# A four-layer convolution kernel: the statistics pass of the quantised convolution reordered by hand, and layer 0's output maximum taken image by image

## The chip, the core and the metric

The kernel runs on one core of one Trainium2 chip. The metric is the device time of one execution in microseconds (us), from the first to the last instruction. A second figure used below is the granted TensorE clock, as a share of full speed, which the profile lists.

The core has five instruction streams. PE (TensorE) multiplies matrices into the accumulator memory PSUM, which has eight banks of 128 x 512 fp32. DVE (VectorE) and ACT (ScalarE) work elementwise. POOL (GpSimd) does cross-partition maxima and memsets here. SP (SyncE) only issues DMA transfers, which 16 DMA engines carry out between HBM and the on-chip memory SBUF. Each stream is executed in its own order and waits on semaphores for the others.

## What is computed

The input x has shape (4, 16, 512, 512): four images of 16 channels. Four layers follow one another.

```python
# layer 0: depthwise 3x3 convolution, windowed attention (8 x 8 windows, 2 heads), MLP, residuals
x = layer0(x)
# layer 1: 8-bit fake quantisation of input and weights, 3x3 convolution, batch norm, clip
step = max(abs(x)) / 127                      # over the whole tensor
xq = clip(round(x / step), -127, 127) * step
y = conv3x3(xq, wq)
mean, var = y.mean(axis=(0, 2, 3)), y.var(axis=(0, 2, 3))
x = clip(y * inv + (beta - mean * inv), 0, 6)  # inv = gamma / sqrt(var + eps)
# layer 2: x + conv3x3(relu(conv3x3(x)))
# layer 3: x + mlp(conv3x3(x)), hidden width 128
```

Layer 1 has two dependences on the whole tensor. The quantisation step needs the largest magnitude of layer 0's output, and the batch norm needs the mean and variance of the convolution's output. So the input of layer 1 is read twice: once for the statistics, once for the result.

## The kernel before

**Layer 0** is `window_attention` (L138). It makes 64 steps. Each step handles a column band 64 wide of all four images; two steps (an even and an odd n) share one input tile and one output tile `xo` of [128, 4 images, 8 rows, 128 columns]. The order of PE, DVE, ACT and SP is written out by hand (`tc.manual_schedule`, L451): what stands first in the program runs first on its engine. Within a step come eight blocks of scores, exponentials and weighted sums (L482 to L498), the projection (L500), and then the MLP of 16 pieces (L510 to L517), between which the depthwise convolution of step n + 2 is spread. `output` (L425) adds the MLP's result to the residual and writes one image's part of `xo` (L430). Its fourth call for a step is made only in the next step, behind that step's first transposes and scores (L477). After both halves, `store` (L435) takes the maximum of |xo| over the whole tile into one column of `peak` with one VectorE reduction (L437), and issues 32 DMAs into the HBM tensor `x1` (L444), eight per image. At the end, a bound on the scores is reduced to a flag (L526 to L537) that SyncE loads (L538); a fallback, `attention_block`, runs only if the flag is zero.

**The statistics pass** is `quant_conv` (L857). Its own order is left to the scheduler. It first quantises the weights: a load of 98 KB (L880), a maximum over the partitions on GpSimd (L872), a step and its reciprocal, and the rounding by adding and subtracting 12582912 (L883, L884). The same function `step_of` turns `peak` into the input's step. Then it walks over 65 tiles `lx` of [128, 4, 512] fp32 (1 MB each; row pairs of the four images, from four strips that lie 128 rows apart). For each tile, `load` (L898) issues four DMAs of 256 KB (L964), scales in place on VectorE (L901), and rounds to bf16 on ScalarE (L902) into one of three ring tiles `lq`. There are three buffers for `lx`. For each of 64 output tiles, 96 small matmuls (L980, four by four at a time on 32 x 32 blocks) convolve two neighbouring ring tiles into four PSUM banks, and four `bn_stats` (L913) read one bank each:

```python
load(0)
for mm in range(M):
    load(mm + 1)
    p = [ps.tile([P, W], F32, tag="p", name=f"lp{mm}_{b}") for b in range(B)]
    for turn in _turns():
        _conv_turn(nc, p, cq, (ring[mm % 3], ring[(mm + 1) % 3]), *turn)
    for b in range(B):
        nc.vector.bn_stats(stats[:, mm * B + b, :], p[b])
```

After the loop the 256 partial statistics are aggregated (L929), summed over the strips with two matmuls (L918), and turned into a `scale` and a `shift` (L947) by a chain of small instructions.

**The tail** is `conv_tail` (L988), again in an order written by hand (L1164, which comes behind the first definitions). It reads `x1` again, quantises tile by tile (`scaled` L1042 on VectorE, `rounded` L1045 on ScalarE, one row of four at a time), and carries the layers 1, 2 and 3 as a pipeline over tiles: `done0` (L1050) applies `scale` and `shift` to the layer 1 convolution and makes z. Two load buffers (tag "x") and two output buffers (tag "o") are in use, each 1 MB, besides rings of padded tiles for the layers' intermediates. It starts with the tiles -2 and -1, which lie partly outside the image, and 0 (L1176).

Of the kernel before, what the change touches and what calls it, by code (L numbers as in the profile page):

```python
# [24 lines left out]
P = 128  # L25
# [75 lines left out]
@with_exitstack  # L101
def conv_chain(ctx: ExitStack, tc: tile.TileContext, x, mats, vecs, cqs, cws, hots, out):
    nc = tc.nc
    const = ctx.enter_context(tc.tile_pool(name="const", bufs=1))
    dram = ctx.enter_context(tc.tile_pool(name="dram", bufs=1, space=DRAM))


    x1 = dram.tile([B, (S + 1) * 2 * M, C, W], F32, name="x1")
    zero = const.tile([C, W], F32, name="zero")
    nc.vector.memset(zero, 0.0)  # L110
    for b in range(B):
        nc.sync.dma_start(x1[b, 0], zero)
        nc.sync.dma_start(x1[b, H + 1], zero)

    mat = const.tile([P, N_MAT], F32, name="mat")
    vec = const.tile([P, N_VEC], F32, name="vec")
    cw = const.tile([P, 3, 2, 3, 32], F32, name="cw")
    nc.sync.dma_start(mat, mats)
    nc.sync.dma_start(vec, vecs)
    nc.scalar.dma_start(cw, cws)  # L120

    def m(name):
        return mat[:, MAT_AT[name]]

    def v(name):
        return vec[:, VEC_AT[name]]

    peak = const.tile([P, HR // WS], F32, name="peak")

    safe = window_attention(tc, x, x1, hots, m, v, peak)  # L130
    with tc.If(safe == 0):
        attention_block(tc, x, x1, m, v, peak)
    quant = quant_conv(tc, x1, const, cqs, m, v, peak)
    conv_tail(tc, x1, out, cw, quant, m, v)


@with_exitstack
def window_attention(ctx: ExitStack, tc, x, x1, hots, m, v, peak):  # L138
# [286 lines left out]
    def output(y, xo, hids, u, half):  # L425
        b = bank(7)
        for vv, hd in hids:
            nc.tensor.matmul(b[quad(vv)], m("fc2"), hd, start=True, stop=True)  # L428
        at = BW * half
        nc.vector.tensor_tensor(  # L430
            xo[:, u, :, at : at + BW].rearrange("p a (j x) -> p a j x", x=WS),
            by_window(b), by_window(y[:, u]), ALU.add,
        )

    def store(xo, k):  # L435
        i, cb = divmod(k, NQ)
        nc.vector.tensor_reduce(  # L437
            peak[:, k : k + 1], xo, AX.XYZ, ALU.max, apply_absolute_value=True
        )
        for u in range(U):  # L440
            for vv in range(V):
                for w in range(2):
                    r = SR * (2 * vv + w) + WS * i
                    nc.sync.dma_start(  # L444
                        x1[u, r + 1 : r + 1 + WS, :, XW * cb : XW * cb + XW].rearrange(
                            "a c x -> c a x"
                        ),
                        xo[32 * vv + C * w : 32 * vv + C * w + C, u],
                    )
# [20 lines left out]
    for n in range(STEPS + 1):  # L470
# [4 lines left out]
        if last:  # L475

            output(*last)  # L477
            if n % 2 == 0:
                store(xo, n // 2 - 1)
# [30 lines left out]
        for i in range(13 * 4):  # L510
            q, rest = divmod(i - 4, 3)
            if i >= 4 and rest == 0 and q < 16:
                hids.append(hidden(y, q, n))
                if q in (5, 9):
                    output(y, xo, hids[q - 5 : q - 1], q // 4 - 1, n % 2)
# [5 lines left out]
        output(y, xo, hids[8:12], 2, n % 2)  # L521
        last = (y, xo, hids[12:], U - 1, n % 2)
# [333 lines left out]
@with_exitstack  # L856
def quant_conv(ctx: ExitStack, tc, x1, const, cqs, m, v, peak):  # L857

    nc = tc.nc
    one = ctx.enter_context(tc.tile_pool(name="l1c", bufs=1))
    rows = ctx.enter_context(tc.tile_pool(name="l1r", bufs=3))
    ps = ctx.enter_context(tc.tile_pool(name="l1p", bufs=8, space=PSUM))

    def step_of(columns, name):

        most = one.tile([P, 1], F32, name=f"most_{name}")
        nc.vector.tensor_reduce(most, columns, AX.X, ALU.max, apply_absolute_value=True)  # L870
        every = one.tile([P, 1], F32, name=f"every_{name}")
        nc.gpsimd.partition_all_reduce(every, most, P, bass_isa.ReduceOp.max)  # L872
        step = one.tile([P, 1], F32, name=f"step_{name}")
        nc.vector.tensor_scalar(step, every, 1.0 / QP, None, ALU.mult)
        inv = const.tile([P, 1], F32, name=f"inv_{name}")
        nc.vector.reciprocal(inv, step)
        return step, inv

    wf = one.tile([P, 6 * 32], F32, name="wf")
    nc.scalar.dma_start(wf, cqs)  # L880
    sw, iw = step_of(wf, "w")
    cq = const.tile([P, 2, 3, 32], BF16, name="cq")
    nc.vector.tensor_scalar(wf, wf, iw, ROUND, ALU.mult, ALU.add)  # L883
    nc.vector.tensor_scalar(  # L884
        cq.rearrange("p s d o -> p (s d o)"), wf, ROUND, None, ALU.subtract
    )
    unround = const.tile([P, 1], F32, name="unround")
    nc.vector.memset(unround, -ROUND)
    sx, ix = step_of(peak, "x")
    stats = one.tile([P, M * B, 6], F32, name="stats")  # L890

    ring = []
    for i in range(3):
        t = one.tile([P, S, WP], BF16, name=f"lq{i}")
        nc.gpsimd.memset(t[:, :, 0 : WP : WP - 1], 0.0)
        ring.append(t)

    def load(mm):  # L898
        t = rows.tile([P, S, W], F32, tag="x", name=f"lx{mm}")
        _load_pairs(nc, t, x1, mm)  # L900
        nc.vector.tensor_scalar(t, t, ix, ROUND, ALU.mult, ALU.add)  # L901
        nc.scalar.activation(  # L902
            ring[mm % 3][:, :, 1 : W + 1], t, AF.Identity, bias=unround
        )

    load(0)
    for mm in range(M):
        load(mm + 1)
        p = [ps.tile([P, W], F32, tag="p", name=f"lp{mm}_{b}") for b in range(B)]
        for turn in _turns():  # L910
            _conv_turn(nc, p, cq, (ring[mm % 3], ring[(mm + 1) % 3]), *turn)
        for b in range(B):
            nc.vector.bn_stats(stats[:, mm * B + b, :], p[b])  # L913


    def over_strips(col, name):
        p = ps.tile([P, W], F32, tag="p", name=f"pm_{name}")
        nc.tensor.matmul(p[:, 0:1], m("same"), col, start=True, stop=True)  # L918
        t = one.tile([P, 1], F32, name=f"os_{name}")
        nc.vector.tensor_scalar(t, p[:, 0:1], 1.0 / NS, None, ALU.mult)  # L920
        return t

    def mul(a, b, name):
        t = one.tile([P, 1], F32, name=f"mul_{name}")
        nc.vector.tensor_tensor(t, a, b, ALU.mult)
        return t

    own = one.tile([P, 2], F32, name="own")
    nc.vector.bn_aggr(own, stats.rearrange("p r s -> p (r s)"))  # L929
    mean = over_strips(own[:, 0:1], "mean")  # L930
    off = one.tile([P, 1], F32, name="off")
    nc.vector.tensor_tensor(off, own[:, 0:1], mean, ALU.subtract)
    spread = one.tile([P, 1], F32, name="spread")
    nc.vector.scalar_tensor_tensor(spread, off, off, own[:, 1:2], ALU.mult, ALU.add)
    var = over_strips(spread, "var")
    s = mul(sx, sw, "s")
    var = mul(mul(var, s, "v1"), s, "v2")
    nc.vector.tensor_scalar(var, var, BN_EPS, None, ALU.add)
    nc.scalar.activation(var, var, AF.Sqrt)
    inv = one.tile([P, 1], F32, name="inv")  # L940
    nc.vector.reciprocal(inv, var)
    inv = mul(inv, v("gamma"), "inv")
    scale = const.tile([P, 1], F32, name="scale")
    nc.vector.tensor_tensor(scale, inv, s, ALU.mult)
    shift = const.tile([P, 1], F32, name="shift")
    ms = mul(mean, scale, "ms")
    nc.vector.tensor_tensor(shift, v("beta"), ms, ALU.subtract)  # L947
    return ix, unround, cq, scale, shift
# [39 lines left out]
def conv_tail(ctx: ExitStack, tc, x1, out, cw, quant, m, v):  # L988
# [16 lines left out]
    ix, unround, cq, scale, shift = quant  # L1005
# [19 lines left out]
    nc.vector.tensor_scalar(edge_b1, v("edge"), v("l2_b1"), None, ALU.mult)  # L1025

# [9 lines left out]
    def load(mm):  # L1036
        loaded[mm] = ld.tile([P, S, W], F32, tag="x", name=f"tx{mm}")
        _load_pairs(nc, loaded[mm], x1, mm)

    def scaled(mm, s):  # L1040
        t = loaded[mm][:, s]
        nc.vector.tensor_scalar(t, t, ix, ROUND, ALU.mult, ALU.add)  # L1042

    def rounded(mm, s):
        nc.scalar.activation(  # L1045
            inner(qs(mm))[:, s], loaded[mm][:, s], AF.Identity, bias=unround
        )

# [92 lines left out]
    def group(conv, unit, between):  # L1141
# [18 lines left out]
        if unit:  # L1160
            waiting.append((*unit, hids))

    ctx.enter_context(
        tc.manual_schedule(  # L1164
            engines={
                mybir.EngineType.PE, mybir.EngineType.DVE, mybir.EngineType.Activation,
                mybir.EngineType.SP,
            }
        )
    )  # L1170

# [4 lines left out]
    for mm in (-2, -1, 0):  # L1176
        load(mm)
        if mm < 0:
            for s in range(S):
                scaled(mm, s)  # L1180
                rounded(mm, s)
    for t in range(-2, M + 7):
        if t + 3 <= M + 2:
            load(t + 3)
        new = [lambda s=s: scaled(t + 2, s) for s in range(S)]
        new += [lambda s=s: rounded(t + 2, s) for s in range(S)]
# [144 lines left out]
```

## Time and profile before

The times of three executions are 6926.55, 6930.18 and 6936.06 us; the median is 6930.18. The profiled execution has a span of 6931.8 us at a mean granted clock of 0.960. By stage:

| stretch (us) | stage | PE busy | DVE busy | ACT busy | clock | DMA share |
|---|---|---|---|---|---|---|
| 0 to 3628.5 | layer 0 | 3511.70 | 1599.29 | 2696.58 | 0.99 | 0.49 |
| 3628 to 4124 | statistics pass | 180.50 | 248.02 | 131.71 | 0.57 | 0.63 |
| 4124 to 6932 | tail | 2768.15 | 1330.46 | 1386.97 | 0.99 | 0.28 |

Some durations that matter, as the medians of their groups:

| instruction | count | one of it (ns) |
|---|---|---|
| scaling of a tile, DVE, L901 | 65 | 1268 |
| rounding of a tile, ACT, L902 | 65 | 2003 |
| bn_stats of a bank, DVE, L913 | 256 | 680 |
| aggregation, DVE, L929 | 1 | 7090 |
| maximum of xo, DVE, L437 | 32 | 4420 |

In the views of the trace, a row gives a start, a duration, the engine, the line in the kernel, what is written and read, and how many instructions were merged; square brackets give the idle time of the engine before it and the work whose end it waited for. Instructions of one group overlap by a little at their ends, so four bn_stats of 680 ns take less than four times that. In the waits, a row says who waited for whom, how long in total, how often, and the longest. In the stretches, the busy time of each engine is followed by the granted clock, the mean busy share of the DMA engines, and the rate in GB/s.

### The profile page before, as it was taken

How to read it: one execution, taken by the hardware profiler on the slowest of the kernel's cores; microseconds unless marked ns; L12 is line 12 of the kernel's file. 1: busy time of each engine (PE TensorE's matmuls, PEld its weight loads, DVE VectorE, ACT ScalarE, POOL GpSimd, SP SyncE). 2: the span in 40 equal slices, each digit the busy share in tenths (PEclk: the TensorE clock that was granted, in tenths of full speed). 3: DMA queues.
4: the chain of work that ended last, by engine and by line, in shares of the span. 5: the costliest groups of instructions: out<-in, count | busy, mean ns of one | idle time of the engine just before them, and what ended most of it. 6: DMA issues, size and time to landing. Idle time of an engine off the chain costs nothing. (4 is left out here: it accounts for less than half of the span.)

```text
span 6931.8 us, 317952 instructions
## 1 busy us (share of the span) xinstructions
PE 6460.4 (93%) x146976; PEld 3307.2 (48%) x146976; DVE 3177.8 (46%) x4550; ACT 4215.3 (61%) x5744; POOL 10.2 (0%) x51
## 2 busy tenths in 40 slices
PE   7999999999999999999983339999999999999999
PEld 4555555555555555555532224444444444444443
DVE  2444444444444444444434454444444444444444
ACT  4777777777777777777762234555555555555553
POOL 0000000000000000000000000000000000000000
PEclk9999999999999999999985559999999999999999
DMA  6455454545545454554327653222223222232221
GB/s 71 63 64 72 63 66 62 66 66 62 70 63 67 63 66 65 64 70 62 51 46 155 144 125 75 76 76 77 83 79 82 76 76 76 76 84 78 82 63 45
DMA packets 759438, 514.79 MB, mean 74 GB/s; under 512 B 354128, under 2 KB 648656, under 8 KB 749904
## 3 DMA queue, kind: packets, MB, share of 16 engines
q1 hardware_dynamic: 757808, 493.95, 40.2%
q8 instruction: 1154, 18.91, 1.3%
q14 instruction: 188, 1.54, 0.1%
q10 hardware_dynamic: 288, 0.39, 0.0%
HBM read 225.28 MB, written 134.48 MB: 52 GB/s over the span
## 5 line engine op out<-in xcount | busy, mean ns | idle before, releaser
L1115 PE MATMUL tb<-y,mat 32*32 32x512 f32 x16384 | 1685.8, 598 | 10.4 <-ACT hid L1121 7.5
L1121 ACT ACTIVATE hid<-tb,vec 128x512 f32<-128x512 f32 x1280 | 877.3, 687 | 1233.5 <-PE tb L1115 1211.7
L368 ACT ACTIVATE e<-pair 128x1024 f32<-128x1024 f32 x1024 | 992.3, 1021 | 231.1 <-PE pair L360 230.4
L1123 DVE TENSOR_SCALAR hid<-tb,vec 128x512 f32<-128x512 f32 x768 | 576.5, 751 | 1169.0 <-PE tb L1115 854.8
L296 PE MATMUL pair<-x,taps 32*32 32x512 f32 x18432 | 1002.9, 608 | 26.9 <-DMA x<-in_x_dram 13.5
L417 PE MATMUL bank<-y,fc_e 32*32 32x512 f32 x8192 | 886.2, 607 | 12.7 <-issue 8.2
L422 ACT ACTIVATE hid<-bank,f1b 128x512 f32<-128x512 f32 x1024 | 679.2, 686 | 327.8 <-PE bank L417 310.0
L352 DVE COPY yt<-bank 128x512 f32<-128x512 f32 x512 | 353.4, 690 | 817.4 <-PE bank L347 817.0
L1115 PEld LDWEIGHTS tb<-y,mat 32*32 32x32 f32 x16384 | 503.8, 103 | 396.5 <-issue 233.3
L360 PE MATMUL pair<-g,y 32*128 32x128 f32 x16384 | 650.5, 285 | 41.1 <-ACT e L368 36.3
L980 PE MATMUL tb<-z,cw 32*32 32x512 f32 x12864 | 642.7, 602 | 3.8 <-issue 2.8
L980 PE MATMUL tb<-x,cw 32*32 32x512 f32 x12480 | 632.9, 597 | 1.8 <-ACT z L1052 1.5
L980 PE MATMUL tb<-h,cw 32*32 32x512 f32 x12672 | 627.0, 599 | 1.6 <-ACT z L1052 1.5
L360 PEld LDWEIGHTS pair<-g,y 32*128 32x128 f32 x16384 | 537.8, 186 | 189.9 <-ACT e L368 107.1
L296 PEld LDWEIGHTS pair<-x,taps 32*32 32x32 f32 x18432 | 450.9, 103 | 356.8 <-issue 234.6
L379 PE MATMUL bank<-e,yt 128*32 128x128 f32 x16384 | 555.9, 276 | 2.4 <-ACT r L394 0.9
L384 PE MATMUL bank<-e,hot 128*32 128x512 f32 x4096 | 535.1, 593 | 0.0
L1129 PE MATMUL tb<-hid,mat 128*32 128x512 f32 x4096 | 498.0, 604 | 0.9 <-DVE o L1135 0.9
L980 PEld LDWEIGHTS <-cq 32*32 32x32 bf16 x12672 | 241.3, 93 | 531.5 <-issue 475.8
L980 PE MATMUL lp<-lq,cq 32*32 32x512 bf16 x6144 | 179.4, 623 | 314.0 <-ACT lq L902 288.8
L379 PEld LDWEIGHTS bank<-e,yt 128*32 128x32 f32 x16384 | 417.9, 109 | 112.1 <-DVE yt L352 60.3
L430 DVE TENSOR_TENSOR xo<-bank,y 128x512 f32<-128x512 f32 x256 | 176.8, 691 | 640.5 <-PE bank L428 639.1
(157 smaller groups left out, 6898.4 us busy)
## 6 DMA issues: line engine op xcount, KB each, us to landing
lx<-x SPq DMA_DIRECT2D x260, 256.0 KB, 5.1
tx<-x SPq DMA_DIRECT2D x260, 256.0 KB, 5.1
y<-y SPq DMA_DIRECT2D x2048, 32.0 KB, 2.1
x<-xo SPq DMA_DIRECT2D x1024, 64.0 KB, 2.1
xi<-x SPq DMA_DIRECT2D x1024, 64.0 KB, 2.7
out_dram<-o SPq DMA_DIRECT2D x64, 1024.0 KB, 4.3
x<-in_x_dram SPq DMA_DIRECT2D x496, 81.2 KB, 6.3
x<-in_x_dram SPq DMA_DIRECT2D x496, 80.6 KB, 6.3
```

What stands on the lines that cost most here:

```text
L296: nc.tensor.matmul(bank(u)[quad(vv)], taps[quad(u), tap, :], xts[n // 2][quad(u), vv, dy : dy + WS, at : at + BW], start=tap == 0, stop=ta ...
L360: nc.tensor.matmul(bank(u)[:, P * jj : P * jj + P], y2[quad(u), vv, jl + jj].rearrange("p w t -> p (w t)"), g[quad(u), vv, jl + jj].rearra ...
L368: nc.scalar.activation(e[:, 2 * i : 2 * i + 2].rearrange("p u j t -> p u (j t)"), pairs[i], AF.Exp,)
L379: nc.tensor.matmul(b[quad(u), P * jj : P * jj + P], yt[:, jj, quad(u)], e[:, u, jj, :], start=True, stop=True,)
L384: nc.tensor.matmul(d[quad(u)], own, e[:, u].rearrange("p j t -> p (j t)"), start=True, stop=True,)
L417: nc.tensor.matmul(b[quad(k)], fc1[quad(vv), quad(k)], y[quad(vv), u, :], start=True, stop=True,)
L422: nc.scalar.activation(hd, b, AF.Gelu, bias=f1b)
L980: nc.tensor.matmul(p[i][_quad(j)], weights[_quad(i), side, dx, :], src[side][_quad(i), j, dx : dx + W], start=side == 0 and dx == 0, stop= ...
L1115: nc.tensor.matmul(p[_quad(c)], w1[_quad(b), 1 - par, 32 * c : 32 * c + 32], inner(ys(mm + par))[_quad(b), s, :], start=True, stop=True,)
L1121: nc.scalar.activation(hd, p, AF.Relu, bias=v("l3_b1"))
L1123: nc.vector.tensor_scalar(hd, p, v("l3_b1"), 0.0, ALU.add, ALU.max)
L1129: nc.tensor.matmul(out_bank[_quad(b), :], w2[:, par], hd, start=par == 0, stop=par == 1)
```

## The change

It has three parts.

First, `quant_conv` is gone. The pass over the statistics now stands at the head of the tail's function, which is called `conv_layers`, inside the order written by hand. It uses the tail's own buffers: tiles are loaded in turn into the tags "x" and "o", four in all; the quantised tiles go into the tail's ring `q` of three; the statistics matmuls use the tail's eight PSUM banks, in two sets of four. Loading runs four tiles ahead, scaling and rounding two tiles ahead of the matmuls. Behind the last tile, the tiles -2 and -1 are loaded, scaled and rounded whole, and tile 0 is loaded, before the statistics are aggregated. This is for having the engines work on different tiles at the same time.

Second, the quantisation of the weights moves to the start of the program, into `quant_weights`, so that nothing of it is left between the layers.

Third, layer 0's `store` is called for each image as soon as `output` has written its second half. Each call takes the maximum over one image's [128, 8, 128] part into a column of its own, so `peak` has 128 columns instead of 32, cleared at the start, and issues the eight stores of that image.

```diff
+    cq, sw = quant_weights(tc, const, cqs)
+    peak = const.tile([P, 4 * HR // WS], F32, name="peak")
+    nc.gpsimd.memset(peak, 0.0)
 ...
-    quant = quant_conv(tc, x1, const, cqs, m, v, peak)
-    conv_tail(tc, x1, out, cw, quant, m, v)
+    conv_layers(tc, x1, out, cw, cq, sw, m, v, peak)
 ...
-    def store(xo, k):
+        if n % 2:
+            store(xo, n // 2, u)
+    def store(xo, k, u):
         i, cb = divmod(k, NQ)
         nc.vector.tensor_reduce(
-            peak[:, k : k + 1], xo, AX.XYZ, ALU.max, apply_absolute_value=True
+            peak[:, U * k + u : U * k + u + 1], xo[:, u], AX.XY, ALU.max,
+            apply_absolute_value=True,
         )
-        for u in range(U):
-            for vv in range(V):
+        for vv in range(V):
 ...
             output(*last)
-            if n % 2 == 0:
-                store(xo, n // 2 - 1)
 ...
+    tags = ("x", "o")
+    for mm in range(4):
+        load(mm, tags[mm % 2])
+    sx, ix = quant_step(nc, act, act, peak, "x")
+    for mm in range(2):
+        scaled(mm)
+        rounded(mm)
+    for mm in range(M):
+        if mm + 4 <= M:
+            load(mm + 4, tags[mm % 2])
+        if mm + 2 <= M:
+            scaled(mm + 2)
+            rounded(mm + 2)
+        p = banks[4 * (mm % 2) : 4 * (mm % 2) + 4]
+        for turn in _turns():
+            _conv_turn(nc, p, cq, (qs(mm), qs(mm + 1)), *turn)
+        for b in range(B):
+            nc.vector.bn_stats(stats[:, mm * B + b, :], p[b])
+    for mm in (-2, -1):
+        load(mm)
+        scaled(mm)
+        rounded(mm)
+    load(0)
 ...
-    for mm in (-2, -1, 0):
-        load(mm)
-        if mm < 0:
-            for s in range(S):
-                scaled(mm, s)
-                rounded(mm, s)
```

The chain from the aggregation to `scale` and `shift` is the same, and stands behind the last lines shown. The loop of the tail over t is unchanged.

## The prediction

> **What bounds the kernel now.** I read the page first: busy shares, then the 40 slices.
>
> ```profile
> PE 6460.4 (93%) x146976; PEld 3307.2 (48%) x146976; DVE 3177.8 (46%) x4550; ACT 4215.3 (61%) x5744; POOL 10.2 (0%) x51
> ...
> PE   7999999999999999999983339999999999999999
> ...
> PEclk9999999999999999999985559999999999999999
> DMA  6455454545545454554327653222223222232221
> ```
>
> TensorE fills the two large stages; what is done to other engines there is mostly free. In slices 21 to 24 every digit falls: this is the statistics pass of layer 1 (L901 to L913), about 3628 to 4124 us. Next, the timeline of one tile in its middle:
>
> ```profile
> 3853.47 2.49 DVE L913 BATCH_NORM_STATS2 stats<-lp 128x6 f32<-128x512 f32 x4 [3.65 <-PE lp L980]
> 3855.88 1.27 DVE L901 TENSOR_SCALAR lx<-lx,inv_x 128x2048 f32<-128x2048 f32 x1
> 3857.23 2.00 ACT L902 ACTIVATE lq<-lx,unround 128x2048 bf16<-128x2048 f32 x1 [5.33 <-DVE lx L901]
> 3859.28 2.79 PE L980 MATMUL lp<-lq,cq 32*32 32x512 bf16 x96 [4.54 <-ACT lq L902]
> ...
> 3860.80 2.49 DVE L913 BATCH_NORM_STATS2 stats<-lp 128x6 f32<-128x512 f32 x4 [3.65 <-PE lp L980]
> ```
>
> This is a closed ring: the statistics of tile k, the scaling of tile k+2, its rounding, the matmuls of tile k+1, its statistics. VectorE works in order and was given scaling behind the statistics, so nothing overlaps. The period is 3860.80 - 3853.47 = 7.33 us. The engines' own work per tile is 2.79 (PE), 2.49 + 1.27 = 3.76 (DVE) and 2.00 (ACT). The critical chain names the load in many tiles, but the waits of SyncE in this stretch show the load waiting for the ring:
>
> ```profile
> SPq L964 <- ACT lq L902: 322.0, 60, 5.5
> SPq L964 <- DVE shift L947: 29.6, 1, 29.6
> ```
>
> Then the busy times by stretch, for what the DMA could do: first the 24 us in which three free buffers were being filled, then the ring.
>
> ```profile
> 3634.00:3658.00 24.00, 7.67 (x240) 4.04 (x240) 8.65 (x11) 6.01 (x3) 0.00 (x0) 0.57 1.07 212
> 3700.00:4100.00 400.00, 151.53 (x5216) 92.61 (x5200) 201.78 (x275) 109.14 (x55) 0.00 (x0) 0.57 0.64 143
> ```
>
> The second last column is the DMA share: saturated at 212 GB/s against 0.64 of it in the ring. A tile is 4 x 256 KB = 1.0486 MB, so 4.95 us at 212 GB/s. Last, the hand-over to the tail, by its timeline:
>
> ```profile
> 4112.47 7.09 DVE L929 BATCH_NORM_AGGREGATE own<-stats 128x2 f32<-128x1536 f32 x1
> ...
> 4123.42 0.16 DVE L947 TENSOR_TENSOR shift<-vec,mul_ms 128x1 f32<-128x1 f32 x1
> ...
> 4139.16 1.68 DVE L1042 TENSOR_SCALAR tx<-tx,inv_x 128x512 f32<-128x512 f32 x4 [4.83 <-DMA tx<-x]
> 4139.68 2.56 ACT L1045 ACTIVATE q<-tx,unround 128x512 bf16<-128x512 f32 x4 [4.16 <-DVE tx L1042]
> 4142.15 2.75 ACT L1052 ACTIVATE z<-tb,shift,scale 128x512 f32<-128x512 f32 x4
> ```
>
> Between `shift` (ready at 4123.58) and the first z lie 18.57 us of loading and rounding tiles -2, -1 and 0.
>
> [...] 2048 elements reduced in 2.274 us and 4096 in 4.420, hence 1.048 ns an element and 0.13 us fixed.
>
> **The change, part by part.**
>
> *Ring removed.* Scaling and rounding run two tiles ahead, so at tile k the rounding of k+1 is one period old. Matmuls k need that and banks freed two tiles ago; two sets of four banks suffice. Work per tile is unchanged, and the bound becomes the largest of DMA 4.95, DVE 3.76, PE 2.79, ACT 2.00. The scaling of k+2 now heads the VectorE queue, with the statistics of k behind it; it waits for a landing. Those statistics release only banks for k+2, nearly two periods off, so this head-of-line wait is harmless. Loads: four buffers instead of three. As built, each load of both programs also waits for the eighth before it, so two tiles are in flight, as in the 24 saturated us. A buffer is released 3.4 us after its landing (1.27 + 2.00 and hand-overs), and its next load isn't due for another period; no wait. SyncE issues a tile's four loads in about 4 x 0.43 = 1.7 us. For the period I have 4.95 from the rate and 5.05 from the landings of the first two tiles (scalings at 3638.28 and 3643.33): I take 5.00, bounds 4.85 (the 216 GB/s of the best 6 us) and 5.3 (198 GB/s, below anything in those 24 us). From the scaling of tile 0 to that of tile 64 before: 4105.02 - 3638.28 = 466.7; after: 64 x 5.00 = 320.0. Saved 146.7.
>
> *End of the pass.* Before, 4105.02 to `shift` at 4123.58 is 18.6 us. After, from the scaling of tile 64: 3.4 to its rounding, 1.5 to the first bank's statistics, 2.5 for four = 7.4; then two memsets (0.48) and two whole-tile scalings (1.27) now stand in VectorE's queue ahead of the aggregation: 3.5, and about 0.4 for tile -1, whose buffer comes free only with tile 64 (+3.4) and whose load took 7.5 before; then 7.1 and 4.0 as before. Sum 22.4: lost 3.8.
>
> *Start of the tail.* Tiles -2 and -1 are rounded and tile 0 loaded behind the aggregation; the convolution of -2 needs no `shift` and hides too. What is left after `shift` is the scaling and rounding of tile 0, 4142.15 - 4139.16 = 2.99 plus 0.2, against 18.57: saved 15.4. From the first z the order is the old one.
>
> *Maximum by image.* 32 reductions of 4096 become 128 of 1024. By the slope, one costs 1.20 us. Three of each four follow their image's addition in the odd step. The first two fall into idle time of VectorE (3.70 us before the second L430, 4.41 us before L311); the third delays a copy of yt (L352, at 1853.04) whose reader (L379) starts 4.4 us later. Cost nothing. The fourth replaces 4.42 us ahead of the copy of yt (L352). In the timeline that copy starts 1.07 us after its transposes in the even step, 0.69 in the odd, and the next matmuls (L379) 1.81 against 1.69: 0.12 us x 31 = 3.7 saved. At the end of layer 0 the flag is ready 3.2 us sooner, but SyncE is issuing stores until 3622.2 and now takes the flag there instead of at 3623.1: 0.9 saved. Store order is unchanged: the first image's stores already start at its addition in before.
>
> *Weights at the start.* Eight small instructions and one load move ahead of the first weight product. As built, `ec`, which starts the chain of PE and DVE products up to the first loads of x at 24.75, now stands behind the cross-partition maximum. `ec` waited until 9.28 for `vec` anyway; that hides a load of 2.5 us and 1.2 us of work. Two more 0.3 us operations lie in the chain. Unknown is the first cross-partition maximum on GpSimd: it took 0.46 us, but any preparation was hidden in 16.5 us of idleness. Bounds 0 and 11; I take 1.0. Clearing `peak` is on idle GpSimd.
>
> Sum: 146.7 - 3.8 + 15.4 + 3.7 + 0.9 - 1.0 = 161.9. 6930.2 - 161.9 = 6768.3.
>
> **The rivals.**
> *A, as worked out: the DMA becomes the bound, 6768.* For it: 24 us at a share of 1.07 with the same loads.
> *B, a lower sustained rate or imperfect overlap, about 6.0 us a tile:* 64 us more, 6832. For it: going from the ring to saturation, the rate per share falls (143/0.64 = 223, 212/1.07 = 198), so packets already hinder each other, and 24 us are short. Against it: no decay within them.
> *C, the DMA does better and VectorE binds at 3.9 us:* 70 us less, 6698. [...] Against: no 6 us show over 216.
> *D, slower than before: the shared buffers or the queue order serialise a tile completely.* Then each pays issue to landing 7.0 (3631.26 to 3638.28), 1.35 and 2.05: 10.4 us, 64 x 3.07 = 197 more, less 16 net of the other parts: 7111. Against it: a buffer has four periods of life, and nothing in the built waits ties a load to the previous tile.
>
> **How the numbers follow.** A 0.82, B 0.08, C 0.06, D 0.03, and 0.01 that an unforeseen cost eats the gain. A, B and C are faster: 0.96; same 0.01; slower 0.03. A alone spans, with the period's bounds, 6759 to 6787; the start's 10 more and layer 0's gain gone give 6802. Below, 9 us more for the hand-over and start: 6750. That leaves out little of A and all of B to D, some 2 in 10.
>
> **What would show it.** Right: a scaling every 5.0 us, DMA share about 1 and 210 GB/s in the pass, VectorE waiting for landings before the scaling, SyncE waiting for earlier loads instead of ACT; `shift` about 340 us after the first scaling; the first z about 3 us after `shift`; layer 0 shorter by 3 or 4 us. Wrong: the matmuls still waiting for ACT in each tile (D), a DMA share well under 1 (B), VectorE without gaps (C), or PE starting much later than 9.6 us at the start.

## The result and the profile after

The changed kernel takes 6781.8 us (median of four executions, 6772.3 to 6789.0). The kernel before, run beside it, takes 6933.1 us. The ratio is 0.9782, with a 95% interval of 0.9765 to 0.9799: 151 us less, by the interval 139 to 163. The forecast was 6768 us, 14 us too low and inside its range.

The page of the kernel after, its busy shares and its 40 slices:

```profile
PE 6456.3 (95%) x146976; PEld 3304.6 (49%) x146976; DVE 3196.5 (47%) x4640; ACT 4215.1 (62%) x5738; POOL 10.3 (0%) x49
...
PE   7999999999999999999995569999999999999999
...
DVE  2444444444444444444444764444444444444444
...
PEclk9999999999999999999996679999999999999999
DMA  6454555545454545455526962222222222322221
```

Every engine has about as much work as before. The hole in the PE row is shorter (slices 22 to 24), and in its middle slice the DMA digit is 9, where no slice of the pass stood above 7 before. A stretch in the middle of the pass confirms it. The columns are the busy times of PE, PEld, DVE, ACT and POOL with counts, the granted clock, the DMA share and the rate in GB/s:

```profile
3700.00:3860.00 160.00, 86.69 (x3147) 53.10 (x3134) 117.58 (x162) 62.78 (x32) 0.00 (x0) 0.63 1.00 210
```

The share is 1.00 at 210 GB/s; in the ring of the kernel before it was 0.64 at 143. The timeline of two tiles of the pass (start, duration, engine, line, operation; in brackets the idle time before it and what ended that):

```profile
3859.35 2.49 DVE L1015 BATCH_NORM_STATS2 stats<-tb 128x6 f32<-128x512 f32 x4
...
3861.43 3.45 PE L914 MATMUL tb<-q,cq 32*32 32x512 bf16 x96 [0.80 <-ACT q L993]
...
3861.76 1.27 DVE L990 TENSOR_SCALAR tx<-tx,inv_x 128x2048 f32<-128x2048 f32 x1
...
3862.95 2.49 DVE L1015 BATCH_NORM_STATS2 stats<-tb 128x6 f32<-128x512 f32 x4
3863.19 2.01 ACT L993 ACTIVATE q<-tx,unround 128x2048 bf16<-128x2048 f32 x1 [1.81 <-DMA tx<-x]
...
3865.35 1.27 DVE L990 TENSOR_SCALAR tx<-tx,inv_x 128x2048 f32<-128x2048 f32 x1
```

The ring is gone: statistics, scaling, rounding and matmuls of different tiles overlap, and here one tile follows the other in 3865.35 - 3861.76 = 3.59 us. But this is not the mean. From the scaling of tile 0 to that of tile 64 it takes 3973.90 - 3645.75 = 328.15 us, 5.13 a tile, against 466.74 before. The intervals range from 3.59 to 9.48 us, where before nearly all of them were 7.33. What interrupts them is in the waits of the pass, here from 3660 to 3970 us (who waited for whom: total, times, longest):

```profile
PE tb L914 <- issue: 129.9, 40, 6.0
ACT q L993 <- DVE tx L990: 92.3, 26, 7.5
DVE stats L1015 <- PE tb L914: 82.4, 34, 5.8
ACT q L993 <- DMA tx<-x: 79.8, 26, 6.4
...
DVE tx L990 <- DMA tx<-x: 6.6, 4, 2.6
```

The first row is new. In 310 us TensorE stood still 40 times for nothing that the profile names ("issue"), 3.2 us each, and VectorE's statistics waited for it. The row with "DMA" for ScalarE misleads: each of the 65 roundings starts at most 0.16 us after the scaling of its own tile has ended, so ScalarE waits for VectorE, not for a load. And by the last row VectorE's scaling found its tile missing only four times. The waits of SyncE in the same stretch:

```profile
SPq L898 <- ACT q L993: 129.9, 50, 7.8
SPq L898 <- DMA tx<-x: 62.2, 76, 2.1
```

So the load queue waits more for ScalarE to give a buffer free than for earlier loads. A DMA share near 1 and loads that keep waiting for compute stand side by side; this is what the experiments had to sort out.

The hand-over to the tail, by its timeline:

```profile
3973.90 1.27 DVE L990 TENSOR_SCALAR tx<-tx,inv_x 128x2048 f32<-128x2048 f32 x1
...
3981.33 1.29 DVE L990 TENSOR_SCALAR tx-2_119520<-tx-2_119520,inv_x 128x2048 f32<-128x2048 f32 x1
...
3983.42 1.28 DVE L990 TENSOR_SCALAR tx-1_119528<-tx-1_119528,inv_x 128x2048 f32<-128x2048 f32 x1 [0.26 <-DMA tx-1_119528<-x]
3984.62 7.08 DVE L1037 BATCH_NORM_AGGREGATE own<-stats 128x2 f32<-128x1536 f32 x1
...
3995.51 0.16 DVE L1055 TENSOR_TENSOR shift<-vec,mul_ms 128x1 f32<-128x1 f32 x1
3995.70 1.67 DVE L990 TENSOR_SCALAR tx<-tx,inv_x 128x512 f32<-128x512 f32 x4
3996.22 2.56 ACT L993 ACTIVATE q<-tx,unround 128x512 bf16<-128x512 f32 x4 [1.51 <-DVE tx L990]
3998.68 2.76 ACT L1060 ACTIVATE z<-tb,shift,scale 128x512 f32<-128x512 f32 x4
```

The scalings of tiles -2 and -1 stand ahead of the aggregation, that of tile 0 behind `shift`. From the scaling of tile 64 (3973.90) to the end of `shift` it takes 21.77 us (18.56 before), and from there to the first z 3.01 (18.57 before).

The two profiled executions, span 6931.8 and 6787.2, differ by 144.6 us. It adds up by stage, to rounding: 138.6 saved between the first and the last scaling, 15.6 at the start of the tail and 1.1 in the rest of it; lost are 3.2 at the end of the pass, 2.0 between the flag and the first scaling, and 5.4 up to the flag. The last term means little. In the profiled executions of eleven versions with this layer 0 the flag is computed anywhere from 3612 to 3633 us. A part that moves layer 0 by a few microseconds can't be read from single profiles.

### The profile page after: what moved, and what is told of

Same layout as the page of the kernel before. It is cut to its first block, busy times and chain, and to the rows that moved or that the text cites. A ratio compares the mean times of both kernels' runs of the same rounds, so it can differ in the third digit from the quotient of the medians.

```text
span 6787.2 us, 317928 instructions
## 1 busy us (share of the span) xinstructions
PE 6456.3 (95%) x146976; PEld 3304.6 (49%) x146976; DVE 3196.5 (47%) x4640; ACT 4215.1 (62%) x5738; POOL 10.3 (0%) x49
## 5 line engine op out<-in xcount | busy, mean ns | idle before, releaser
L1123 PE MATMUL tb<-y,mat 32*32 32x512 f32 x16384 | 1682.9, 597 | 10.4 <-ACT hid L1129 7.5
L418 PE MATMUL bank<-y,fc_e 32*32 32x512 f32 x8192 | 890.9, 609 | 10.4 <-issue 6.3
L914 PE MATMUL tb<-q,cq 32*32 32x512 bf16 x12672 | 468.2, 483 | 185.0 <-issue 130.8
L993 ACT ACTIVATE q<-tx,unround 128x512 bf16<-128x512 f32 (+1 forms) x333 | 313.8, 967 | 235.4 <-DVE tx L990 131.9
```

Source lines behind the costliest of these rows:

```text
L418: nc.tensor.matmul(b[quad(k)], fc1[quad(vv), quad(k)], y[quad(vv), u, :], start=True, stop=True,)
L914: nc.tensor.matmul(p[i][_quad(j)], weights[_quad(i), side, dx, :], src[side][_quad(i), j, dx : dx + W], start=side == 0 and dx == 0, stop= ...
L1123: nc.tensor.matmul(p[_quad(c)], w1[_quad(b), 1 - par, 32 * c : 32 * c + 32], inner(ys(mm + par))[_quad(b), s, :], start=True, stop=True,)
```

## The experiments

Where "stretch" is said below, it is 3700 to 3860 us of each kernel's trace, with the columns explained above.

### Layer 0's part, alone and undone

`e_l0_alone` is the kernel before with the third part of the change only; `e_l0_undone` is the kernel after without it.

```diff
 e_l0_alone, on the kernel before
+        if n % 2:
+            store(xo, n // 2, u)
...
-            peak[:, k : k + 1], xo, AX.XYZ, ALU.max, apply_absolute_value=True
+            peak[:, U * k + u : U * k + u + 1], xo[:, u], AX.XY, ALU.max,
+            apply_absolute_value=True,
...
-            if n % 2 == 0:
-                store(xo, n // 2 - 1)
```

> The kernel before with the layer 0 part of the change alone (maximum and stores image by image, 128 columns of peak cleared at the start); statistics pass and weights as before. The prediction's step (a fourth reduction of 1.2 us in place of 4.42 ahead of the copy of yt, and the flag taken 0.9 us sooner): 4.6 us faster, ratio 0.9993. The rival, read from the trace after, where layer 0 reached its flag 5.4 us later: the part costs up to 5 us, ratio 1.0007. If both are within the noise of layer 0, the interval holds 1.

Measured: 6932.1 against 6940.2 us, ratio 0.9986, interval 0.9980 to 0.9993. The interval, taken of 6940 us, is a saving of 5 to 14 us, 9.7 at its middle. The rival, that it costs time, falls; the 4.6 us of the forecast lie just below the interval, so the part seems to do more than I had counted.

> The changed kernel with layer 0's store put back to one maximum and 32 stores a tile, everything else as changed. If the layer 0 part saves 4.6 us: 4.6 us slower than the changed kernel, 6786. If the part costs 5 us: 6777. If it does nothing: 6782.

Measured: 6799.2 us, ratio 0.9791 (0.9778 to 0.9805), against 0.9782 of the kernel after. This is 6 us in the same direction, but the intervals overlap, so alone it would show nothing.

### What breaks the ring: how far ahead the quantisation runs

`e_one_ahead` keeps the hand-written order, the four buffers and the eight banks, and scales and rounds one tile ahead instead of two.

```diff
-    for mm in range(2):
-        scaled(mm)
-        rounded(mm)
+    scaled(0)
+    rounded(0)
 ...
-        if mm + 2 <= M:
-            scaled(mm + 2)
-            rounded(mm + 2)
+        scaled(mm + 1)
+        rounded(mm + 1)
```

> The changed kernel with scaling and rounding one tile ahead of the matmuls instead of two, four load buffers and the hand-written order kept. Theory (the depth breaks the ring on VectorE): the period returns from 5.13 to about 7.33 us a tile, the total to about 6782 + 64 x 2.2 = 6923, SyncE waits for ACT again, DMA share in the pass 0.65. Rival (buffers or the hand-written order bring the gain): period about 5.1, total about 6782.

Measured: 6917.8 us in a single execution (the kernel before, beside it: 6940.2), 7.36 us a tile. Its stretch:

```profile
3700.00:3860.00 160.00, 61.09 (x2112) 37.39 (x2081) 80.48 (x110) 42.08 (x21) 0.00 (x0) 0.56 0.64 145
```

The share of 0.64 and the 145 GB/s are those of the kernel before. The statistics of tile k, then the scaling and rounding of k + 1, then its matmuls form the ring again. So nearly all of the gain of the pass comes from the distance of two tiles, and none to speak of from the order by hand or the buffers by themselves.

### What bounds the pass now: loads taken away

`e_no_loads2` loads no tile behind tile 4; a tile's buffer is scaled and rounded again with the same work, so VectorE, ScalarE and TensorE do what they did. `e_no_loads` was meant to be the same but, other than its expectation says, also left out ScalarE's rounding from the fifth tile on; it took 6688.6 us in a single execution, at 3.6 us a tile in the stretch.

```diff
+    def again(mm):
+        t = loaded[mm]
+        op = ALU.subtract if mm // 4 % 2 else ALU.add
+        nc.vector.tensor_scalar(t, t, one, ROUND, ALU.mult, op)
...
-            load(mm + 4, tags[mm % 2])
-        if mm + 2 <= M:
+            loaded[mm + 4] = loaded[mm]
+        if 4 <= mm + 2 <= M:
+            again(mm + 2)
+            rounded(mm + 2)
+        elif mm + 2 <= M:
```

> The changed kernel without the statistics pass's loads beyond the first four tiles: the four buffers are scaled and rounded again and again with an instruction of the same kind and size, so the statistics are not those of the input; the tail loads as before. Theory (the DMA is what binds the pass at 5.13 us a tile): VectorE becomes the bound at 3.8 to 3.9, the total falls by 64 x 1.3 = 83 to about 6700, and TensorE no longer idles 3 us every 128 matmuls if that idling comes from instruction transfers queued on the busy DMA engines. Rival (the pass is held by the engines' hand-overs or by TensorE's idling by itself): period 4.8 to 5.1, total 6765 to 6782.

> As e_no_loads, but with the rounding on ScalarE kept for every tile (e_no_loads left it out along with the loads, from the fifth tile on). The statistics are again not those of the input. Theory (the DMA binds): ScalarE's 2.0 us a tile hide behind VectorE's 3.59, so the period stays 3.6 and the total about 6690. Rival (it was the rounding, not the loads, that made the difference): period back at 4.5 to 5.1, total 6745 to 6782.

Measured for `e_no_loads2`: 6677.5 us in a single execution. Its stretch, and the instruction queue in its DMA view (packets, MB, share):

```profile
3700.00:3860.00 160.00, 90.36 (x4224) 59.86 (x4224) 159.17 (x221) 88.87 (x45) 0.00 (x0) 0.81 0.01 4
```

```profile
q8 instruction: 33, 0.54, 1.3%
```

VectorE is busy for 159.17 of 160 us, at 3.6 us a tile. So it is the loads that keep the kernel after 1.5 us a tile above what VectorE needs. By which wait they do it is another question, since without them TensorE's waits for "issue" are gone too. In the same stretch of the kernel after, these are the waits of TensorE and VectorE that count:

```profile
PE tb L914 <- issue: 68.3, 21, 6.0
...
DVE stats L1015 <- PE tb L914: 45.4, 18, 4.7
```

No scaling waits there for a landing; VectorE's idle time lies before the statistics, which wait for matmuls. So by the trace, in most tiles the loads do not hold the pass up by landing late. They hold it up by way of TensorE.

The second fence of `e_no_loads2` points at what TensorE waits for. In these 160 us it took 4224 matmuls, and 33 packets of 16 KB came over the queue that the view calls "instruction": one packet per 128 matmuls, with their 128 weight loads. From kernel to kernel the packets of this queue follow the matmuls: in the same stretch 24 for 3147 in the kernel after, 14 for 1776 in `e_half_matmuls` and 12 for 1440 in `e_by_strip`, which follow below. No wait of PE for "issue" appears without loads. In the kernel after, all 41 waits of PE for "issue" in the pass lie exactly 128 matmuls apart, or a multiple of that. There the packets share the DMA engines with a load queue that fills 98.3% of them, and in the stretch, which had 24 such packets in it, TensorE has 21 of these waits, 68.3 us in all. That they are waits for the packets is argued from the counts, from the distance of 128 and from their absence without loads; no run changed the packets by themselves, so it is not shown.

### Half of the matmuls

`e_half_matmuls` computes one side of the convolution only, 48 matmuls a tile; all loads are kept.

```diff
-        for turn in _turns():
-            _conv_turn(nc, p, cq, (qs(mm), qs(mm + 1)), *turn)
+        for dx in range(3):
+            for i in range(4):
+                for j in range(4):
+                    nc.tensor.matmul(p[i][_quad(j)], cq[_quad(i), 1, dx, :],
+                        qs(mm + 1)[_quad(i), j, dx : dx + W],
+                        start=dx == 0, stop=dx == 2)
```

> The changed kernel with only one of the two sides of each convolution in the statistics pass, 48 matmuls a tile instead of 96, so the statistics are those of half a convolution; all loads are made. [...] Theory (the irregular rhythm and the 0.1 us a tile over what the loads' 208 GB/s allow come from TensorE's stalls every 128 matmuls): stalls half as many, scalings more even, period 5.05 instead of 5.13, total 5 us less, 6777. Rival (the stalls are hidden and the DMA alone sets 5.13): the total stays within 2 us of 6782, apart from run-to-run noise of several us; the period in the trace decides.

Measured: 6731.5 us in a single execution, and a pass of 285.0 us instead of 328.2. I had expected much less. Its stretch in four parts:

```profile
3700.00:3740.00 40.00, 13.60 (x432) 6.22 (x432) 30.54 (x42) 16.12 (x9) 0.00 (x0) 0.50 1.06 222
3740.00:3780.00 40.00, 12.09 (x384) 5.51 (x384) 31.82 (x45) 17.66 (x9) 0.00 (x0) 0.50 1.06 230
3780.00:3820.00 40.00, 13.60 (x432) 6.22 (x432) 33.58 (x47) 18.43 (x10) 0.00 (x0) 0.50 1.06 250
3820.00:3860.00 40.00, 16.12 (x528) 7.62 (x528) 37.72 (x52) 20.05 (x10) 0.00 (x0) 0.50 1.03 272
```

The share is full from beginning to end, and the rate climbs from 222 to 272 GB/s. So a full share isn't a fixed rate: the same packets of the same loads get through faster. SyncE no longer waits for ScalarE at all in the stretch (it waits 109.1 us there, all for earlier loads), so the queue never runs dry. And here the landings do set the pace:

```profile
DVE tx L990 <- DMA tx<-x: 25.4, 29, 2.1
```

VectorE's scaling waits for its tile 29 times in the stretch, and TensorE not once for "issue", though the share is as full as before; 14 instruction packets came instead of 24, and TensorE waited 107.8 us for ScalarE, time in which a wait for a packet may go unseen. So these loads can land at 4.45 us a tile on the mean, and the 5.13 of the kernel after isn't their limit alone: TensorE's stalls are in it. That opened two questions: whether the buffers or the memory layout hold the loads back, and whether it matters where in SBUF the loads in flight go.

### Fewer tiles in flight, longer runs

`e_three_buffers` loads three tiles ahead instead of four. `e_layout` lays `x1` out so that a partition's four rows are one run of 8 KB, where they were four runs of 2 KB that lie 4 MiB apart; layer 0's stores and the other loads follow it.

```diff
 e_three_buffers
-    tags = ("x", "o")
+    tags = ("x", "o", "x")
-        if mm + 4 <= M:
-            load(mm + 4, tags[mm % 2])
+        if mm + 3 <= M:
+            load(mm + 3, tags[mm % 3])
 e_layout
-    x1 = dram.tile([B, (S + 1) * 2 * M, C, W], F32, name="x1")
+    x1 = dram.tile([B, 2 * M, C, S + 1, W], F32, name="x1")
```

> The changed kernel with three load buffers in the statistics pass instead of four (order and depth of the quantisation kept). Theory (a buffer is free 3.4 us after its landing and two tiles of loads are in flight anyway, so three suffice): period 5.1 to 5.2, total 6782 to 6788. Rival (the fourth buffer carries the gain): each buffer's cycle of release, load and landing, 3.4 + 7.5 + 5 us over three tiles, period 5.3 to 6, total 6795 to 6840.

Measured: 6796.3 us in a single execution, 335.8 us for the pass. The total is just on the rival's side, but the kernel before, run beside it, took 6942.9 us, 9.8 more than beside the kernel after; as a ratio it is 0.979, against 0.978. The pass is 7.7 us longer than the kernel after's; that of `e_l0_undone`, which is the same pass, took 332.9, so single traces differ by 5 us here. The fourth tile in flight helps a little at most, and is not what the rate hangs on (206 GB/s with three).

> The changed kernel with x1 laid out so that a partition's four rows of a tile lie together (8 KB in one run) instead of four runs of 2 KB, 4 MiB apart; 64 of layer 0's 1024 stores are cut in two by it. Theory (the pass is bound by how fast the DMA engines read x1, and the short runs 4 MiB apart are what keeps them at 211 GB/s): the rate rises to 290 GB/s or more, VectorE becomes the bound at 3.6 to 3.8 us a tile, the pass is 64 x 1.4 = 90 us shorter, total about 6690, ratio 0.965. Rival (211 GB/s is the rate of these transfers whatever the layout): total 6782, ratio 0.978.

Measured: 6777.2 us, ratio 0.9762 (0.9746 to 0.9779). The stretch:

```profile
3700.00:3860.00 160.00, 86.19 (x3183) 51.83 (x3183) 121.49 (x167) 66.18 (x33) 0.00 (x0) 0.66 0.96 214
```

214 GB/s instead of 210, where the theory had named 290, and 318.6 us for the pass. The times of the two kernels can't be told apart, so neither the pitch nor the length of the runs is what keeps the loads near 210 GB/s; an effect of a few per cent is not excluded.

### Where the loads in flight go

Images 0 and 1 lie in partitions 0 to 63 of a tile, images 2 and 3 in 64 to 127. The kernel after issues image by image, so two transfers to one half are followed by two to the other, and its loads run at 210 GB/s in the stretch. Three kernels keep the bytes and change where neighbours go. That the rate would rise with both halves in flight was my assumption; no trace up to here had shown it.

`e_interleave` issues the images in the order 0, 2, 1, 3; `e_two_queues` issues images 2 and 3 from ScalarE's queue.

```diff
 e_interleave
-            load(mm + 4, tags[mm % 2])
+            load(mm + 4, tags[mm % 2], (0, 2, 1, 3))
...
-    for b in range(B):
+    for b in order:
 e_two_queues
-        nc.sync.dma_start(
+        (nc.scalar if two and b > 1 else nc.sync).dma_start(
```

> After, with one edit: in the statistics pass the four transfers of a tile are issued in the order of images 0, 2, 1, 3 instead of 0, 1, 2, 3, still on one queue. Images 0 and 1 go to partitions 0 to 63, images 2 and 3 to partitions 64 to 127. Theory ([...] the run with half of the matmuls reached 272 to 290 GB/s[...]): neighbours now lie in opposite halves, the rate rises to 235 GB/s or more, the mean period falls from 5.13 to 4.4 us or less (ratio to before 0.974 or less, 6752 us or less). Rival ([...] the rate is set by how often the queue runs empty): the rate stays within 208 to 222 GB/s and the time within 6770 to 6790 us.

> After, with one edit: in the statistics pass images 0 and 1 of a tile are loaded from SyncE's queue as now, images 2 and 3 from ScalarE's queue, each issued just ahead of the rounding of tile m+2. Theory [...]: [...] 235 GB/s or more and 6752 us or less, as with the order 0, 2, 1, 3 or better. Rival ([...] the sum of bytes sets the time): 208 to 222 GB/s and 6770 to 6790 us. A third way: ScalarE issues its share only when it comes by, after its wait for VectorE, so its loads start later than SyncE's would and the time is above 6790 us.

Measured: `e_interleave` 6751.8 us (6750.5 to 6752.4), ratio 0.9731 (0.9715 to 0.9748). `e_two_queues` 6772.5 us, ratio 0.9766 (0.9748 to 0.9785). First the stretch of `e_interleave`, then that of `e_two_queues`:

```profile
3700.00:3860.00 160.00, 89.84 (x3299) 53.30 (x3289) 124.20 (x172) 70.18 (x35) 0.00 (x0) 0.64 1.01 231
```

```profile
3700.00:3860.00 160.00, 84.08 (x3008) 50.17 (x2979) 115.64 (x159) 62.15 (x31) 0.00 (x0) 0.63 1.01 213
```

The order of four statements is worth 29 us of the pass: 231 GB/s at the same share, and 298.9 us. TensorE's waits for "issue" in the stretch fell with it, from 68.3 us to 52.0. So the order of issue matters. That it does because neighbours then lie in opposite halves is not shown: the order also changes the sequence in which the images are read from HBM, and no run parts the two. The second queue, which was also meant to have both halves in flight, did not do it. Its rate, 213 GB/s, is what the rival expected, the sum of bytes at the old rate; its pass is 315.1 us, and its ratio can't be told from the kernel after's.

`e_one_transfer` fills each tile from the fifth on with one transfer of 1 MB over all 128 partitions, of other rows than the convolution needs.

```diff
-            load(mm + 4, tags[mm % 2])
+            whole(mm + 4, tags[mm % 2])
+    def whole(mm, tag):
+        loaded[mm] = ld.tile([P, S, W], F32, tag=tag, name=f"tx{mm}")
+        at = 8 * (mm % M)
+        nc.sync.dma_start(
+            loaded[mm], x1[:, at : at + 8].rearrange("b r c w -> (r c) b w"))
```

> After, with the loads of the statistics pass from tile 4 on replaced: each tile is filled by one transfer of 1 MB over all 128 partitions (8 rows x 16 channels of each of the 4 images, runs of 2 KB as now) instead of four transfers of 256 KB over 32 partitions each. The bytes are the same, the rows are not the ones that the convolution needs, so the statistics and the output are of other data; everything else is after. Theory [...]: [...] 280 GB/s or more, the period falls to VectorE's 3.6 to 3.9 us and the time to 6690 to 6720 us. Rival (the rate is set by the queue running empty while the buffers wait for TensorE's stalls, not by where the bytes go): 211 to 240 GB/s, 4.5 to 5.1 us, 6745 to 6785 us.

Measured: 6696.2 us, ratio 0.9653 (0.9637 to 0.9669); the pass takes 244.3 us. Its stretch, and then two of the waits between 3660 and 3900 us:

```profile
3700.00:3860.00 160.00, 102.00 (x4080) 61.24 (x4080) 153.91 (x213) 85.11 (x43) 0.00 (x0) 0.71 0.85 283
```

```profile
ACT q L993 <- DVE tx L990: 83.9, 46, 3.9
...
PE tb L914 <- issue: 26.3, 17, 2.5
```

283 GB/s at a share of 0.85, VectorE busy for 153.91 of 160 us, and TensorE's waits for "issue" down to 26.3 us in 240 us. It is nearly as in the kernel without loads: VectorE binds. The DMA view gives the packets of the load queue, first in the stretch of the kernel after, then of this one (packets, MB, share of 16 engines):

```profile
q1 hardware_dynamic: 18191, 33.12, 98.3%
```

```profile
q1 hardware_dynamic: 22533, 44.74, 83.8%
```

A packet occupied its engine for 0.983 x 16 x 160 / 18191 = 138 ns in the kernel after and for 95 ns here, though it carries 1821 and 1985 bytes on the mean. In the same way `e_interleave` has 128 ns and `e_two_queues` 138. So in the kernel after each packet held its engine longer than it has to.

This kernel changed two things at once, the partitions covered and the size of a transfer. `e_by_strip` was to part them, with the right rows and 256 KB as in the kernel after: one transfer for each strip over 128 partitions, instead of one for each image over 32.

```diff
-    for b in range(B):
-        rows = x1[b, at : at + 2 * M * (s1 - s0)]
-        nc.sync.dma_start(
-            t[_quad(b), s0:s1],
...
+    for s in range(s0, s1):
+        row = at + 2 * M * (s - s0)
+        nc.sync.dma_start(
+            t[:, s], x1[:, row : row + 2].rearrange("b r c w -> b (r c) w"))
```

> After, with every tile of the statistics pass and of the tail loaded in four transfers of 256 KB as now, cut the other way: one transfer per strip over all 128 partitions (one run of 2 KB in each) instead of one per image over 32 partitions (four runs of 2 KB in each). Same bytes, same rows, same number and size of transfers, one queue; nothing is left out. Theory [...]: 265 GB/s or more in the pass, a period of 3.6 to 3.9 us, 6690 to 6715 us. Rival (what the one transfer of 1 MB brought came from its size or from the fewer issues): 208 to 240 GB/s, 4.5 to 5.2 us, 6745 to 6790 us.

Measured: 7141.4 us, ratio 1.0300 (1.0286 to 1.0314), slower than both kernels, which neither side had expected. Its stretch:

```profile
3700.00:3860.00 160.00, 41.83 (x1440) 25.68 (x1440) 56.14 (x77) 30.93 (x16) 0.00 (x0) 0.52 0.27 100
```

A share of 0.27 is 4.3 of 16 engines, at 100 GB/s, and 10.6 us a tile. The source of each load now has the four images as its first dimension. No run varied that dimension alone, so what holds the share down is not shown. Thus the run tells nothing on size against partitions; what it shows is that a cut of the same bytes left the engines busy for 0.27 of the time, where the kernel after has 1.00. A packet took 84 ns here.

### What is settled and what is open

Settled: without its loads the pass runs at VectorE's rate, and with them it does not; how far it stays above is not decided by their bytes, pitch or runs, but by how they are cut and in which order they are issued. With the same bytes, the pass takes 328, 299 or 244 us. By the waits in the stretch, the pass of the kernel after is held up mostly through TensorE's stalls (68.3 us, none of a scaling for a landing), that of `e_half_matmuls` through landings (25.4 us, no stall). Open: whether the stalls are waits for the instruction packets, which is argued; why the order 0, 2, 1, 3 helps; and how much of `e_one_transfer`'s gain comes from covering all partitions at once and how much from the larger transfer. Open as well: why the rate of `e_half_matmuls` climbs from 222 to 272 GB/s. Its 244 GB/s over the whole stretch, with transfers to 32 partitions in the order 0, 1, 2, 3, show that a queue that never runs dry got beyond the 210 of the kernel after without another order or a larger transfer.

## Why the prediction was right, point by point

**What binds.** Rival A, the loads becoming the bound, was given 0.82. Its numbers came true: share 1.00 and 210 GB/s, where about 1 and 210 had been named, and without loads a tile takes 1.5 us less. But two of its signs did not come. VectorE was to wait for landings before the scaling, and did so 4 times in 310 us; SyncE was to wait for earlier loads instead of ScalarE, and waited 62.2 us for them and 129.9 for ScalarE. In most tiles the wait that ended last was TensorE's, which the forecast did not have. That the period still came out within 3% of the forecast is in part luck. Rival B (6.0 us a tile) and D (10.4 us) did not come. Rival C named VectorE as the next bound, at 3.9 us; without the loads it is 3.6, since the four statistics and the scaling overlap at their ends (in the timeline of the kernel after, by 0.08 us at each of the two joints: 2.49 + 1.27 - 0.16 = 3.60).

**Ring removed.** Forecast 5.00 us a tile and 146.7 us saved; measured 5.13 and 138.6. This is the term that was mis-sized most, and inside its bounds of 4.85 and 5.3. The rate was taken from 24 us at the start of the kernel before, and it held: 212 there, 210 in the stretch. But two sentences of the step were wrong. "No wait" for the buffers: SyncE waited 129.9 us for ScalarE to release them, twice as long as for earlier loads. And that VectorE's wait at the head of its queue is harmless left out TensorE, which was counted at 2.79 us a tile and held to have slack. With the DMA share at 1.00 in the stretch, it stood still 3.2 us at a time; the statistics behind it came late, and the scaling behind those. `e_half_matmuls` shows that TensorE had a hand in the rate. With half of its matmuls the same loads landed at 4.45 us a tile. The step took the share of 1 for a fixed limit; it was a rate of this cut and order of the loads, with TensorE's stalls in it.

**End of the pass.** Forecast 22.4 us from the last scaling to `shift`, measured 21.77. Right.

**Start of the tail.** Forecast 3.2 us from `shift` to the first z, measured 3.01; saved 15.6 against 15.4. Right, for the reason given: the hand-over timeline shows -2 and -1 scaled ahead of the aggregation and only tile 0 behind `shift`.

**Maximum by image.** One reduction took 1.22 us, forecast 1.20. The part saves 9.7 us alone (5 to 14) and 6 by the undone run, against 3.7 + 0.9. The sign was right and the size too small. Where the rest comes from was not found: layer 0 differs more from one execution to the next than the part is worth.

**Weights at the start.** Forecast a loss of 1.0 with bounds 0 and 11. `ec` starts at 9.54 us, 9.28 before: 0.3 lost. The feared preparation of GpSimd's first maximum does not exist here; it took 0.35 us.

**From the flag to the first scaling.** It takes 17.2 us instead of 15.2. The sum of the forecast has no term for it. The step on layer 0 implies one, since it has the flag ready 3.2 us sooner but taken only 0.9 sooner; yet `e_l0_alone`, which has this step too, takes 15.5. The cause stays open, and 16.3 to 19.1 us in other versions with the same code up to there say how little a single trace tells.

The sum of the measured stages without layer 0 is 138.6 - 3.2 + 15.6 - 2.0 - 0.3 = 148.7 us. With 6 to 10 for layer 0 it is 155 to 159, inside the 139 to 163 of the measured ratio. The forecast of 161.9 was high by the 8.1 us of the period above all.

## What to carry to other kernels

When a ring of engines is broken open, read the new bound from the rate of the loads as they are cut and ordered, and treat a DMA share of 1 as a question, not as a limit: here the same bytes ran at 210, 231 and 283 GB/s. Then ask which wait ends last: with the share at 1, the scaling hardly ever waited for a landing. Try the cheap edits first, such as the order in which transfers to different partitions are issued: it gave `e_interleave`, whose ratio to before of 0.9731 (0.9715 to 0.9748) lies below the 0.9782 (0.9765 to 0.9799) of the kernel after, with nothing left out. And look at the waits of TensorE for "issue" where the DMA queues are full: here they took 68.3 of 160 us.

## What the runs showed of the hardware that was not expected

- A busy share of 1 on all DMA engines did not fix the rate: 210 GB/s in the kernel after and 231 with the images in the order 0, 2, 1, 3. A packet of some 1.8 to 2 KB held its engine for 138 ns on the mean in the first, 128 in the second, and 95 with one transfer over 128 partitions (share 0.85).
- In the kernel after, with the load queue full, TensorE stood still nearly once for each 16 KB packet of the instruction queue (21 waits, 24 packets), 3.2 us on the mean and up to 6.0, and always 128 matmuls or a multiple of that apart. It did not without loads (0 waits, 33 packets), nor with a full queue and half of the matmuls (0 waits, 14 packets).
- Two issuing queues instead of one left the rate at 213 GB/s (210 with one).
- Transfers of 256 KB over 128 partitions, whose source has the four images as its first dimension, left the share at 0.27, by which 4.3 of 16 engines were busy on the mean, at 100 GB/s; the cause is not shown.
- Layer 0, the same work in every version, ended anywhere between 3612 and 3633 us in single profiled executions.
